# Inner layer norm of a four-layer graph network: statistics from ScalarE's running sums instead of VectorE's bn_stats, and T^T from VectorE's transposes

## The chip, the cores and the metric

The kernel runs on one core of a Trainium2 chip, as one launch. The metric is the device time of the launch in microseconds. An engine name stands for one of the core's five: TensorE (PE in the profile; its weight loads are PEld), VectorE (DVE), ScalarE (ACT), GpSimd (POOL) and SyncE (SP), which issues the DMA transfers.

## The reference

The input is x, 128 graphs of 64 nodes with 512 features, and adj, one 64 x 64 matrix for each graph, partly zero. All values are fp32. Four layers follow each other, each of the form x = x + L(relu(layernorm(x)), adj):

```python
# layer 0: two hypergraph convolutions with an inner layer norm
h = jax.nn.relu(hypergraph_conv(x, adj, W1, b1))      # 512 -> 1024
h = layer_norm(h, gamma, beta)                        # over the 1024: the "inner" one
y = hypergraph_conv(h, adj, W2, b2)                   # 1024 -> 512
return y + x
# layer 1: attention weights from s = (h @ w) @ a, out = A @ h @ w
# layer 2: softmax-like weights adj * exp(q k^T), times values
# layer 3: K = 3 hops
alpha_matrix = A * jnp.exp(e)
transition = alpha_matrix / (jnp.sum(alpha_matrix, axis=-1, keepdims=True) + 1e-12)
for k in range(Wk.shape[0]):
    H = H + Xk @ Wk[k] + bk[k]
    Xk = jnp.einsum('bij,bjd->bid', transition, Xk)
return jax.nn.relu(H)
```

The layer norms are (x - mean) / sqrt(variance + 1e-5), over the last axis.

## The kernel before

**Tiles and groups.** Two graphs make a tile of 128 rows; T = 4 tiles make a group, and there are 16 groups. Layers 0 and 1 run over all groups; their result goes to DRAM (xm), the weights of layers 2 and 3 replace the first ones in SBUF, and layers 2 and 3 run over all groups. A 64 x 64 matrix of two graphs stands in a 128 x 128 tile ("bd") as two blocks on the diagonal with zeros beside them.

**Products.** Large products go through `strassen` (L577), a form with seven products for eight over a pair of tiles, which emits four result quarters in the order (0,0), (1,1), (1,0), (0,1). Its matmuls stand on L595, those of the similar scheme of layer 2 on L818. A matmul of fp32 shows as two records in the profile.

**The inner layer norm (layer0, L661).** For a pair of tiles, `strassen` with W1 gives z, 128 x 1024 for each tile, in halves of 512. `emit_z` writes a half with VectorE (L615) and applies Relu in place on ScalarE (L707). When both halves of a tile are there, `norm_stats` (L504) runs bn_stats on each (L508) and bn_aggr (L509) on VectorE, and variance + eps and its power of -0.5 on GpSimd (L510, L511). ScalarE scales each half by that (L718; the mean is not subtracted, it is folded into W2). Each half is then transposed: ScalarE splits the words into 16-bit planes (L543), a DMA transposes them (L544) back onto z, ScalarE joins them in rT (L545). `strassen` with W2 (part "q") reads rT. The slots of z are two, so a pair's z must be read before the next pair's is written. The outer layer norms use the same `norm_stats`, through `pre_stats` (L514).

**T and T^T (layer3, L889).** VectorE makes T, the transition matrices of the four tiles, as the diagonal blocks of tr (L908). TensorE transposes each of the four 128 x 128 tiles (L915) into PSUM, ScalarE copies that to tt[:, :, 0, :] (L917). Then TensorE multiplies T by that (L921) and ScalarE copies the result to tt[:, :, 1, :] (L923), the transpose of T squared. The left multiplication `lm` (L936) multiplies h of one graph by its 64 columns of both planes at once, and ScalarE copies that into a3 (L940), the input of the product with the three hops' weights W3.

**What sets the order.** The program isn't written in the order of its text. Every operation is recorded in a `Graph` (L40) with an engine and an assumed cost. `run` (L82) then plays the five engines against each other: of the operations that can start first on an engine, the one with the lowest priority number goes. A priority is the group's time (`PERIOD1` or `PERIOD2` for each group), plus the work passed so far (`step`, times `STRETCH` of the layer), plus a constant of the part (`AT`; `part` sets it). Buffers of a tag (`SLOTS`, `TWO`) are handed out as this play finds them free. The resulting order is fixed in the program, and each engine keeps to it on the chip.

**Lines the prediction uses.** L469: setup products of Wq and Wk from tmp tiles. L534: left multiplication of a tile by a diagonal-block matrix. L679: the matrix M of layer 0. L731: y of layer 0. L844: scores of layer 2. L879, L882: its values and the reciprocal of the row sums. L525: the outer norm's ACTIVATE. L372: a dot product along a row, with VectorE's accumulator. L668: the 0/1 matrix of adj. L387 and the lines before it: sums of weights for `strassen`.

Of the kernel before, what the change touches and what calls it, by code (L numbers as in the profile page):

```python
# [18 lines left out]
T = 4  # L19
# [142 lines left out]
def tile_adj_preln_d4(  # L162
# [25 lines left out]
        ([("tmp", [P, D], 4), ("mB", [P, T, C + 1], 1)], [("s3", [P, 3, 6, P], 1)]),  # L188
        ([("z", [P, DH], 2)], [("hT", [P, KD, T * P], 1)]),
        ([("rT", [P, KH, P], 3)], [("a3", [P, 3 * KD, P], 2)]),  # L190
        ([("s2", [P, 3, 4, P], 1), ("s1", [P, 3, 2, P], 2)], [("vu", [P, 2, D + 1], 2), ("tt", [P, T, 2, P], 1)]),
        ([("y", [P, D], 2)], [("qT", [P, 2, 2 * P], 2)]),
        ([("mT", [P, KD, P], 3)], [("a3", [P, 3 * KD, P], 1)]),
        ([("row", [P, D], 5)], [("sh", [P, 4, 2, 2 * P], 1), ("q", [P, D], 1)]),
# [72 lines left out]
    def quad(b):  # L267
# [1 line left out]

    STRETCH, PERIOD1, PERIOD2 = (2.01, 1.52, 3.8, 3.15), 99.32, 100.99
    AT = {
        "x0": -1000.31, "apart": -0.04, "w1": -1140.59, "b1": -730.1, "w2": -692.69, "w": 166.49, "c1": -856.63,
        "l0": -580.98, "c2": -741.75, "l1": 111.32, "c": 219.34, "g0": -1134.91, "g1": -1116.26, "g2": -755.63,
        "g3": -850.44, "g": -1126.24, "l3": 28.03, "wg": 119.55, "w3": 191.39, "last": -98.19, "load1": -120.84,
        "load2": -92.69, "m": -52.0, "h0": -37.33, "p0": -2.35, "z0": -2.26, "q0": 25.57, "y0": -29.58, "h1": -39.25,
        "p1": -17.85, "z1": 10.94, "q1": 12.3, "y1": 27.38, "s": -11.54, "t0": 62.66, "e0": -103.04, "t1": 54.99,
        "e1": -32.68, "hT": -26.23, "sh": 50.82, "lq": 16.73, "pt": 40.17, "v": -3.1, "pv": -184.92, "s3": 16.54,
        "tt": 62.29, "a0": 61.26, "b0": -39.87, "a1": 81.07, "b1_": 65.71,  # L280
    }

    def part(name):
# [377 lines left out]
    def layer0(g):  # L661
# [28 lines left out]
        for t0 in (0, 2):  # L690
            mh, zs, ys, rTs, k = [], [], [], [], t0 // 2
            part(f"h{k}")
            for t in (t0, t0 + 1):
                xx = xt[g, t]
                h = pre_ln(g, t)
                pool(1.43, lambda xx=xx, h=h: nc.gpsimd.tensor_add(xx.t, xx.t, h.t), [h, xx], [xx])
                pool(1.39, lambda xx=xx: nc.gpsimd.tensor_add(xx.t, xx.t, b2_b.t), [xx, b2_b], [xx])
                mh.append(left_mul_T(h, lambda t=t: M.t[:, t, :], Mr, "mT"))
                zs.append(Buf("z"))
                ys.append(Buf("y"))  # L700
                rTs.append(Buf("rT"))
                step(0.9)

            def emit_z(i, j, p, u, v, t0=t0, zs=zs):
                z, cols, t = zs[i], slice(j * D, (j + 1) * D), t0 + i
                scaled(lambda: z.t[:, cols], (z, j), lambda: rd.t[:, t:t + 1], [rd], lambda: b1_b[j].t, [b1_b[j]], p, u, v, D)
                act(0.63, lambda: nc.scalar.activation(z.t[:, cols], z.t[:, cols], AF.Relu), [(z, j)], [(z, j)])  # L707

            part(f"p{k}")
            strassen(lambda i, j, mh=mh: mh[i].t[:, 2 * j:2 * j + 2, :], {(i, j): [mh[i]] for i in range(2) for j in range(2)},  # L710
                     W1, 2, D, "s1", emit_z)
            part(f"z{k}")
            for i in range(2):
                z, rT = zs[i], rTs[i]
                rs = norm_stats(lambda k, z=z: z.t[:, k * D:(k + 1) * D], 2, [(z, 0), (z, 1)])[1]
                for j in range(2):
                    half = lambda z=z, j=j: z.t[:, j * D:(j + 1) * D]
                    act(0.7, lambda half=half, rs=rs: nc.scalar.activation(half(), half(), AF.Copy, scale=rs.t), [(z, j), rs], [(z, j)])  # L718
                    transposed(half, [(z, j)], Buf("tmp"), half, [(z, j)], lambda rT=rT, j=j: rT.t[:, j * KD:(j + 1) * KD, :], [(rT, j)])
                    step(0.1)  # L720

            def emit_y(i, j, p, u, v, ys=ys):
                biased(ys[i], j, p, u, v, lambda: bw2_b.t, bw2_b)

            part(f"q{k}")
            strassen(lambda i, j, rTs=rTs: rTs[i].t[:, j * KD:(j + 1) * KD, :], {(i, j): [(rTs[i], j)] for i in range(2) for j in range(2)},
                     W2, 4, D // 2, "s2", emit_y)
            part(f"y{k}")
            for i in range(2):
                xx, y, pf, t = xt[g, t0 + i], ys[i], Buf("ps"), t0 + i  # L730
                pe(c_mm(512, 1), lambda y=y, pf=pf, t=t: nc.tensor.matmul(pf.t, M.t[:, t, :], y.t, start=True, stop=True), [(y, 0), (y, 1), *Mr], [pf])  # L731
                dve(0.75, lambda pf=pf, xx=xx, t=t: nc.vector.scalar_tensor_tensor(
                    xx.t, pf.t, rd.t[:, t:t + 1], xx.t, op0=ALU.mult, op1=ALU.add), [pf, rd, xx], [xx])
                step(0.9)
# [154 lines left out]
    def layer3(g):  # L889
# [16 lines left out]
        dve(0.18, lambda: nc.vector.reciprocal(rn.t, dn.t), [dn], [rn])  # L906
        for s in HALVES:
            dve(0.42, lambda s=s: nc.vector.tensor_mul(tr.t[s, :, s], z.t[s], rn.t[s, :, None].to_broadcast([C, T, C])), [z, rn], [(tr, s.start)])  # L908
        trk, pt, p2 = [(tr, 0), (tr, C)], Buf("ps"), Buf("ps")

        part("tt")

        def mt():
            for t in range(T):
                nc.tensor.transpose(quad(pt)[:, t, :], tr.t[:, t, :], ident)  # L915
        pe(KD * TR, mt, trk, [pt])
        act(0.59, lambda: nc.scalar.copy(tt.t[:, :, 0, :], quad(pt)), [pt], [(tt, 0)])  # L917

        def m2():
            for t in range(T):  # L920
                nc.tensor.matmul(quad(p2)[:, t, :], tr.t[:, t, :], tt.t[:, t, 0, :], start=True, stop=True)  # L921
        pe(c_mm(128, T), m2, [*trk, (tt, 0)], [p2])
        act(0.59, lambda: nc.scalar.copy(tt.t[:, :, 1, :], quad(p2)), [p2], [(tt, 1)])  # L923
        step(2.0)
        for t0 in (0, 2):
            part("a0" if t0 == 0 else "a1")
            for t in (t0, t0 + 1):
                h, b, back = pre_ln(g, t, stats[t]), a3[t], Buf("q")
                transposed(lambda h=h: h.t, [h], Buf("o"), lambda back=back: back.t, [back], lambda b=b: b.t[:, :KD, :], [(b, 0)])

                pq = [Buf("ps"), Buf("ps")]

                def lm(h=h, pq=pq, t=t):
                    for c in range(KD):
                        for i, half in enumerate(HALVES):
                            nc.tensor.matmul(quad(pq[i])[:, c, :], h.t[half, c * P:(c + 1) * P], tt.t[half, t, :, half],  # L936
                                             start=True, stop=True)
                pe(c_mm(128, KD) + 0.2, lm, [h, (tt, 0), (tt, 1)], pq)
                for i, half in enumerate(HALVES):
                    act(0.59, lambda pq=pq, b=b, i=i, half=half: nc.scalar.copy(  # L940
                        b.t[:, KD:, half].rearrange("p (j c) k -> p c j k", j=2),
                        pq[i].t.rearrange("p (c j k) -> p c j k", c=KD, j=2)), [pq[i]], [(b, 1 + i)])
                step(1.0)
# [131 lines left out]
```

## Time and profile before

| | |
|---|---|
| time, median of 3 runs (lowest, highest) | 2401.43 us (2398.42, 2402.01) |
| span of the profiled run | 2395.1 us |
| granted TensorE clock in it | 0.998 |
| bn_stats of z: busy, number | 86.2 us, 128 |
| bn_stats of x: busy, number | 174.1 us, 256 |
| TensorE's transposes of T: number, median | 64, 273 ns |
| ScalarE's copies of T^T: number, mean | 16, 585 ns |

The page gives busy time, share of the span and number of instructions of each engine; below that the span in 40 slices, a digit being the busy share in tenths. The durations of matmuls overlap, since they are pipelined and their ends are modelled: how long a matmul holds TensorE is read from the starts of neighbours. A group of instructions is one line, engine and operation with its tiles; after the bar stand its busy time, the mean of one, and the engine's idle time before it with what ended most of that. In a list of waits, the numbers are the total in us, how often, and the longest.

### The profile page before, as it was taken

To read this page: it belongs to the slowest core of one execution; us is meant where nothing else is said; L and a number is where in the kernel's file an instruction comes from. 1 tells how busy PE (TensorE), PEld (TensorE's weight loads), DVE (VectorE), ACT (ScalarE), POOL (GpSimd) and SP (SyncE) were. 2 spreads that over 40 slices of the span, in tenths; PEclk is the share of its full clock that TensorE was granted. 3 is DMA by queue.
4 is the path that set the end of the run, shared out by engine and by line. 5 is a ranking of instruction groups with operands and counts; after the bars stand their busy time and mean duration, and the time that the engine had idled before them with its cause. 6 is when DMAs were issued, how large, how long until landed. Compare 5 with 4: busy or idle time off the path is not lost.

```text
span 2395.1 us, 33543 instructions
## 1 busy us (share of the span) xinstructions
PE 2356.3 (98%) x11930; PEld 1855.0 (77%) x11930; DVE 1721.2 (72%) x3676; ACT 1263.5 (53%) x1754; POOL 938.2 (39%) x1450
## 2 busy tenths in 40 slices
PE   7999999999999999999999999999999999999999
PEld 3576677776777776777778888888888888888887
DVE  7887878787878787877878556666666666666664
ACT  2666565566565566565745445544445444454431
POOL 5234455434455434455344333333333333333321
PEclk9999999999999999999999999999999999999999
DMA  7232222232223222222532232222322222222211
GB/s 242 54 80 47 65 68 71 68 78 51 65 66 73 67 80 52 61 67 77 146 89 62 66 74 55 69 56 58 78 64 60 66 50 71 73 56 64 52 42 36
DMA packets 335928, 168.78 MB, mean 70 GB/s; under 512 B 284688, under 2 KB 290832, under 8 KB 335760
## 3 DMA queue, kind: packets, MB, share of 16 engines
q1 hardware_dynamic: 335760, 166.63, 28.0%
q8 instruction: 94, 1.54, 0.3%
q14 instruction: 74, 0.61, 0.1%
HBM read 64.76 MB, written 34.70 MB: 42 GB/s over the span
## 4 chain that ended last, share of the span: by engine, by line
PE 84%; DVE 6%; DMA 4%; ACT 2%; POOL 2%; issue 2%; SPq 0%; DVEq 0%; POOLq 0%; ACTq 0%
PE ps L595 60%; PE ps L818 11%; PE ps L534 4%; PE ps L936 2%; PE ps L731 2%; PE ps L879 2%; DVE s_s_vu_tt L869 1%; DMA x<-xm 1%; PE ps L844 1%; ACT o L543 1%; DVE bd L854 1%; ACT h L525 1%; POOL u L867 1%; POOL rs L511 1%; DVE st L508 1%
## 5 line engine op out<-in xcount | busy, mean ns | idle before, releaser
L525 ACT ACTIVATE h<-x,nm,rs 128x512 f32<-128x512 f32 x384 | 307.1, 813 | 456.5 <-POOL nm L518 455.3
L595 PE MATMUL ps<-wb_mem,rT_a 128*128 128x256 f32 x2056 | 476.8, 380 | 1.7 <-DVE z_hT L615 0.9
L595 PEld LDWEIGHTS ps<-wb_mem,rT_a 128*128 128x128 f32 x2056 | 386.5, 190 | 74.8 <-issue 20.3
L510 POOL TENSOR_SCALAR rs<-mv 128x1 f32<-128x1 f32 x320 | 101.5, 317 | 534.2 <-DVE mv L509 452.9
L595 PE MATMUL ps<-wb_mem,s_s_vu_tt 128*128 128x256 f32 x1152 | 275.0, 379 | 0.2 <-DVE s_s_vu_tt L587 0.2
L595 PE MATMUL ps<-wb_mem,tmp_mB_s 128*128 128x256 f32 x1152 | 261.3, 379 | 0.2 <-DVE tmp_mB_s L587 0.2
L595 PEld LDWEIGHTS ps<-wb_mem,s_s_vu_tt 128*128 128x128 f32 x1152 | 218.5, 190 | 43.1 <-issue 10.5
L595 PE MATMUL ps<-wb_mem,mT_a 128*128 128x256 f32 x1016 | 240.7, 380 | 1.8 <-ACT u L563 1.3
L595 PEld LDWEIGHTS ps<-wb_mem,tmp_mB_s 128*128 128x128 f32 x1152 | 217.6, 190 | 29.6 <-DVE tmp_mB_s L587 0.6
L595 PE MATMUL ps<-wa_mem,mT_a 128*128 128x512 f32 x512 | 238.0, 593 | 2.1 <-DVE u L567 2.1
L949 POOL TENSOR_TENSOR u<-u,bk_b 128x256 f32<-128x256 f32 x96 | 76.2, 799 | 352.3 <-DVE u L567 292.6
L511 POOL TENSOR_TENSOR rs<-rs,mhalf 128x1 f32<-128x1 f32 x320 | 202.9, 634 | 26.6
L595 PEld LDWEIGHTS ps<-wb_mem,mT_a 128*128 128x128 f32 x1016 | 190.6, 190 | 28.6 <-ACT u L563 1.5
L508 DVE BATCH_NORM_STATS2 st<-x 128x6 f32<-128x512 f32 x256 | 174.1, 680 | 32.4 <-DMA x<-xm 30.8
L595 PE MATMUL ps<-wa_mem,s_s_vu_tt 128*128 128x512 f32 x384 | 182.9, 599 | 1.0 <-ACT c_b L453 0.6
L595 PEld LDWEIGHTS ps<-wa_mem,mT_a 128*128 128x128 f32 x512 | 96.0, 190 | 105.4 <-issue 92.5
L565 DVE TENSOR_TENSOR u<-ps,u 128x256 f32<-128x256 f32 (+1 forms) x160 | 84.4, 527 | 112.1 <-PE ps L595 84.6
L623 POOL TENSOR_TENSOR u<-u,row_sh_q 128x256 f32<-128x256 f32 x96 | 70.9, 746 | 235.0 <-DVE u L565 205.9
L545 ACT COPY rT_a<-z_hT 128x1024 uint16<-128x1024 uint16 x128 | 144.3, 1161 | 4.4 <-DMA z_hT<-tmp_mB_s 4.2
L534 PEld LDWEIGHTS ps<-bd,h 128*128 128x128 f32 x1024 | 129.0, 192 | 16.1 <-issue 8.6
L707 ACT ACTIVATE z_hT<-z_hT 128x512 f32<-128x512 f32 x128 | 79.8, 625 | 116.7 <-DVE z_hT L615 116.6
L563 ACT COPY u<-ps 128x256 f32<-128x256 f32 (+1 forms) x160 | 72.5, 453 | 129.7 <-PE ps L818 71.5
(172 smaller groups left out, 4317.1 us busy)
## 6 DMA issues: line engine op xcount, KB each, us to landing
x<-in_x_dram SPq DMA_DIRECT2D x64, 256.0 KB, 2.8
xm<-x SPq DMA_DIRECT2D x64, 256.0 KB, 2.0
x<-xm SPq DMA_DIRECT2D x64, 256.0 KB, 2.7
out_dram<-x SPq DMA_DIRECT2D x64, 256.0 KB, 2.2
adj<-in_adj_dram SPq DMA_DIRECT2D x32, 256.0 KB, 4.1
rw<-row SPq DMA_DIRECT2D x96, 64.0 KB, 2.8
wb_mem<-in_Wk_dram SPq DMA_DIRECT2D x6, 512.0 KB, 4.4
wa_mem<-in_W1T_dram SPq DMA_DIRECT2D x2, 1024.0 KB, 5.9
```

What stands on the lines that cost most here:

```text
L508: dve(0.69, lambda i=i: nc.vector.bn_stats(st.t[:, i, :], src(i)), [r[i]], [(st, i)])
L510: pool(0.3, lambda: nc.gpsimd.tensor_scalar_add(rs.t, mv.t[:, 1:2], EPS), [mv], [rs])
L511: pool(0.65, lambda: nc.gpsimd.tensor_tensor(rs.t, rs.t, mhalf, ALU.pow), [rs], [rs])
L525: act(0.82, lambda: nc.scalar.activation(h.t, xx.t, AF.Relu, bias=nm.t, scale=rs.t), [xx, nm, rs], [h])
L534: nc.tensor.matmul(quad(p)[:, c, :], h.t[:, c * P:(c + 1) * P], rhs(), start=True, stop=True)
L545: act(1.16, lambda: nc.scalar.copy(u16(dst()).rearrange("p c (k q) -> p c k q", q=2), u16(back()).rearrange("p (q c r) -> p c r q", q=2, c ...
L563: act(n / 1200 + 0.17, lambda: nc.scalar.copy(at(0)(), p1.t[:, :n]), [p1], [(U, 0)])
L565: dve(c_v(n), lambda: nc.vector.tensor_add(at(1)(), p2.t[:, :n], at(0)()), [p2, (U, 0)], [(U, 1)])
L595: nc.tensor.matmul(p.t[:, :n], lhs()[:, c, :], rhs(c), start=first and c == 0, stop=c == kc - 1, skip_group_check=True)
L707: act(0.63, lambda: nc.scalar.activation(z.t[:, cols], z.t[:, cols], AF.Relu), [(z, j)], [(z, j)])
L818: nc.tensor.matmul(pair(p.t)[:, o, :], a, b, start=first and o == 0 and c == 0, stop=c == 1, skip_group_check=True)
L949: pool(0.88, lambda: nc.gpsimd.tensor_add(U.t[:, iv], U.t[:, u[1]], add()), [u, ka], [v])
```

## The change

The statistics of the inner norm move from VectorE to ScalarE and GpSimd. The Relu of each half of z now also gives the half's sum (`accum_out`). GpSimd adds the two sums and divides by -1024, which is minus the mean. Two Squares on ScalarE, with that as the bias, write their result to a scrap tile and give the sums of squared distances; GpSimd adds these, divides, adds eps and takes the power -0.5. VectorE's bn_stats and bn_aggr on z are gone; those of the outer norms stay.

T^T is made by VectorE: a 64 x 64 block is transposed as four blocks of 32 x 32, the two off the diagonal changing places, for four tiles in one instruction. It goes from SBUF to SBUF, without TensorE, PSUM and ScalarE. tt now holds 64 columns for a tile, both graphs below each other, instead of 128, and has two slots instead of one in the same room. The product that gives the transpose of T squared has 64 columns instead of 128.

The planner's constants (STRETCH, PERIOD1, PERIOD2 and all of AT) are other numbers, so the order of the whole program differs.

```diff
-        ([("s2", [P, 3, 4, P], 1), ("s1", [P, 3, 2, P], 2)], [("vu", [P, 2, D + 1], 2), ("tt", [P, T, 2, P], 1)]),
+        ([("s2", [P, 3, 4, P], 1), ("s1", [P, 3, 2, P], 2)], [("vu", [P, 2, D + 1], 2), ("tt", [P, T, 2, C], 2)]),
...
-    STRETCH, PERIOD1, PERIOD2 = (2.01, 1.52, 3.8, 3.15), 99.32, 100.99
+    STRETCH, PERIOD1, PERIOD2 = (2.04, 0.7, 3.87, 2.94), 97.36, 106.92
...
+            zsum = [Buf("col"), Buf("col")]
...
-                act(0.63, lambda: nc.scalar.activation(z.t[:, cols], z.t[:, cols], AF.Relu), [(z, j)], [(z, j)])
+                act(0.65, lambda: nc.scalar.activation(z.t[:, cols], z.t[:, cols], AF.Relu, accum_out=zsum[i].t[:, j:j + 1]), [(z, j)], [(z, j), (zsum[i], j)])
...
-                rs = norm_stats(lambda k, z=z: z.t[:, k * D:(k + 1) * D], 2, [(z, 0), (z, 1)])[1]
+                sm, nm, rs = zsum[i], Buf("nm"), Buf("rs")
+                pool(0.3, lambda sm=sm, nm=nm: nc.gpsimd.tensor_add(nm.t, sm.t[:, 0:1], sm.t[:, 1:2]), [(sm, 0), (sm, 1)], [nm])
+                pool(0.3, lambda nm=nm: nc.gpsimd.tensor_scalar(nm.t, nm.t, -1.0 / DH, None, op0=ALU.mult), [nm], [nm])
+                for j in range(2):
+                    junk = Buf("o")
+                    act(0.65, lambda z=z, j=j, sm=sm, nm=nm, junk=junk: nc.scalar.activation(
+                        junk.t, z.t[:, j * D:(j + 1) * D], AF.Square, bias=nm.t, accum_out=sm.t[:, 2 + j:3 + j]), [(z, j), nm], [junk, (sm, 2 + j)])
+                pool(0.3, lambda sm=sm, rs=rs: nc.gpsimd.tensor_add(rs.t, sm.t[:, 2:3], sm.t[:, 3:4]), [(sm, 2), (sm, 3)], [rs])
+                pool(0.3, lambda rs=rs: nc.gpsimd.tensor_scalar(rs.t, rs.t, 1.0 / DH, EPS, op0=ALU.mult, op1=ALU.add), [rs], [rs])
+                pool(0.65, lambda rs=rs: nc.gpsimd.tensor_tensor(rs.t, rs.t, mhalf, ALU.pow), [rs], [rs])
...
-        trk, pt, p2 = [(tr, 0), (tr, C)], Buf("ps"), Buf("ps")
+        trk, p2 = [(tr, 0), (tr, C)], Buf("ps")
+        B = C // 2
+        def blocks(s):
+            for i in range(2):
+                for j in range(2):
+                    nc.vector.transpose(tt.t[s.start + j * B:s.start + (j + 1) * B, :, 0, i * B:(i + 1) * B],
+                                        tr.t[s.start + i * B:s.start + (i + 1) * B, :, s.start + j * B:s.start + (j + 1) * B])
+        for i, s in enumerate(HALVES):
+            dve(1.2, lambda s=s: blocks(s), [(tr, s.start)], [(tt, 2 + i)])
...
-        def mt():
-            for t in range(T):
-                nc.tensor.transpose(quad(pt)[:, t, :], tr.t[:, t, :], ident)
-        pe(KD * TR, mt, trk, [pt])
-        act(0.59, lambda: nc.scalar.copy(tt.t[:, :, 0, :], quad(pt)), [pt], [(tt, 0)])
...
-                nc.tensor.matmul(quad(p2)[:, t, :], tr.t[:, t, :], tt.t[:, t, 0, :], start=True, stop=True)
-        pe(c_mm(128, T), m2, [*trk, (tt, 0)], [p2])
-        act(0.59, lambda: nc.scalar.copy(tt.t[:, :, 1, :], quad(p2)), [p2], [(tt, 1)])
+                nc.tensor.matmul(p2.t[:, t * C:(t + 1) * C], tr.t[:, t, :], tt.t[:, t, 0, :], start=True, stop=True)
+        pe(c_mm(64, T), m2, [*trk, (tt, 2), (tt, 3)], [p2])
+        act(0.38, lambda: nc.scalar.copy(tt.t[:, :, 1, :], p2.t[:, :T * C].rearrange("p (t c) -> p t c", t=T)), [p2], [(tt, 1)])
...
-                            nc.tensor.matmul(quad(pq[i])[:, c, :], h.t[half, c * P:(c + 1) * P], tt.t[half, t, :, half],
+                            nc.tensor.matmul(quad(pq[i])[:, c, :], h.t[half, c * P:(c + 1) * P], tt.t[half, t, :, :],
```

In the changed kernel the product with T stands on L937 and the new transposes on L928.

## The prediction

> **What bounds the kernel now.** I first read the page's head: busy shares and the 40 slices.
>
> ```profile
> span 2395.1 us, 33543 instructions
> PE 2356.3 (98%) x11930; PEld 1855.0 (77%) x11930; DVE 1721.2 (72%) x3676; ACT 1263.5 (53%) x1754; POOL 938.2 (39%) x1450
> ...
> PE   7999999999999999999999999999999999999999
> ```
>
> TensorE works nearly without a break; VectorE, which the change relieves most, is at 72%. So a saving on VectorE counts only where VectorE makes TensorE wait. To see where that happens I asked for busy time by stretch: start-up, layers 0 and 1, their hand-over to layers 2 and 3, these, and the end.
>
> ```profile
> 0.00:100.00 100.00, 83.41 (x280) 43.94 (x281) 78.49 (x152) 35.81 (x53) 45.62 (x64) 0.98 0.54 166
> 100.00:1150.00 1050.00, 1049.73 (x4415) 759.50 (x4414) 836.42 (x1855) 648.41 (x915) 482.57 (x750) 1.00 0.27 66
> 1150.00:1300.00 150.00, 140.15 (x806) 118.49 (x804) 118.55 (x250) 78.35 (x106) 64.47 (x102) 0.99 0.39 104
> 1300.00:2290.00 990.00, 985.51 (x5894) 850.22 (x5892) 632.07 (x1310) 475.47 (x645) 324.78 (x506) 1.00 0.28 64
> 2290.00:2396.00 106.00, 97.54 (x543) 82.86 (x541) 55.66 (x113) 25.48 (x36) 20.75 (x30) 0.99 0.13 34
> ```
>
> After the stretch's length the columns are PE, PEld, DVE, ACT and POOL busy time. TensorE's idle time is 16.6, 0.3, 9.9, 4.5 and 8.5 us. In layers 0 and 1 it is 0.3 us of 1050: there the new statistics can win nothing, only lose. What a change can win lies in TensorE's own instructions, at the start, at the hand-over and at the end. The list of TensorE's waits agrees: for VectorE's T (L908) it waited once, 1.9 us, and longest for a first load.
>
> ```profile
> PE ps L469 <- DMA tmp_mB_s<-in_Wk_dram: 10.4, 2, 9.5
> PE ps L879 <- DVE ve L882: 4.6, 15, 0.3
> ...
> PE ps L915 <- DVE bd L908: 1.9, 1, 1.9
> ```
>
> The rows that the change touches, from the groups (busy us, mean ns of one, then idle time before):
>
> ```profile
> L508 DVE BATCH_NORM_STATS2 st<-z_hT 128x6 f32<-128x512 f32 x128 | 86.2, 675 | 22.4 <-ACT z_hT L707 22.4
> L707 ACT ACTIVATE z_hT<-z_hT 128x512 f32<-128x512 f32 x128 | 79.8, 625 | 116.7 <-DVE z_hT L615 116.6
> L718 ACT ACTIVATE z_hT<-z_hT,rs 128x512 f32<-128x512 f32 x128 | 91.7, 718 | 50.8 <-POOL rs L511 48.8
> ```
>
> And the timeline of TensorE in one group of layer 3 (start, duration), transposes first:
>
> ```profile
> 1687.38 0.60 PE L915 MATMUL ps<-ident,bd 128*128 128x128 f32 x4
> 1687.81 2.75 PE L595 MATMUL ps<-wb_mem,rT_a 128*128 128x256 f32 x12
> 1690.40 1.05 PE L921 MATMUL ps<-s_s_vu_tt,bd 128*128 128x128 f32 x8
> ```
>
> Durations of matmuls overlap, starts do not: the four transposes hold TensorE from 1687.38 to 1687.81, 0.43 us.
>
> **What the Trainium skill says.** "TensorE: Matmul & The Clock Gate", Part 1: warm matmuls start N / 2.4 GHz + 2.5 ns apart, and an idle array begins at half clock. An fp32 product here is two records, and for N = 256 they start 216 ns apart, twice the stated 109; so fp32 pays two passes per record. The first 12 records, 8.2 us from 9.52 to 17.70, show the cold clock. "ScalarE: Activation LUTs", What ACT_TABLE_LOAD costs: 186 ns + 0.833 N with immediates, 93 ns more for each pointer operand. For N = 512 that is 612, 705, 798; the trace has 625 (L707), 718 (L718), 813 (L525). It agrees. "VectorE: DVE Perf Modes", Two Vector instructions with no wait between them: an instruction whose input or output starts in another group of 32 partitions is held until the earlier ones are done. The new transposes change groups from one to the next, so I let them run end to start; no row of before shows one.
>
> **Part by part: the statistics.** Out go 128 bn_stats x 0.68 us = 86 us and 64 bn_aggr x 0.18 = 12 us of VectorE. In come 128 Squares on ScalarE, one pointer operand like L718, 0.72 each = 92 us, and for 256 sums an unknown price: VectorE's read of an accumulator took 0.08 (L372); I take 0.1 and keep 0 and 0.2. ScalarE gains 92 + 26 = 118 us over some 1180 us (L707's rows run to the hand-over), from about 62% to 72% busy. GpSimd gets three more one-column operations per z tile, 64 x 3 x 0.3 = 58 us, from 46% to 51%. No engine becomes fuller than TensorE.
>
> The wait it adds: ScalarE's Square waits for GpSimd's mean, which waits for ScalarE's last Relu; behind it in ScalarE's queue stand the copies of mT and of the next z. For W2's first product the path from the last W1 product gets longer by two GpSimd operations (0.65 with gaps), up to four Squares (2.9) and one more GpSimd operation (0.3), less bn_stats and bn_aggr (0.9): 3.0 us. How much room is there? In TensorE's order before, between the last W1 product of a pair of tiles and the first W2 product of that pair stand 12.9 us (625.77 to 638.68 in the group I followed) and 13.1 us for the other pair, and TensorE waited for neither. In the changed order I count, with a W1 or W2 product at 1.72, a y product at 0.86, a W product at 0.86 and a left multiplication at 0.89: five W2, two y, three W1 products and one left multiplication, 16.4 us, and for the other pair 30.3. So 3.0 longer stands against 3.5 more room, with the old slack on top: cost 0. The 98 us taken from VectorE lie beside TensorE's work as well: gain 0.
>
> **T^T.** TensorE loses 64 transposes at 0.109 (0.43 / 4): **7.0 us**, all on the path. The multiplication behind them now has N = 64 for 128. L679 with N = 65 held TensorE 0.83 us for eight records (629.21 to 630.04), L921 with N = 128 0.90 (1690.40 to 1691.30): 0.07 per group, 1 us in all, if anything; I take 0. ScalarE loses 16 copies x 0.59 and has shorter second ones, hidden.
>
> VectorE gets 128 transposes of 32 x 128 elements, eight per group, all between T and the multiplication. From below: L668 (64x256, 0.31) less 128 elements at 0.96 GHz, 0.18. From above: a whole 64x256 operation, 0.42 (L908). L908 fits 256 / 0.96 GHz + 0.15; with 128 elements that is 0.29, which I take: 2.3 us per group. T was ready 18.5 us after the last attention product (L879) in most groups, but 20.05, 19.43, 19.78 and 19.02 in four. Two VectorE operations leave that stretch in the new order (0.25 net of ScalarE's Exp, which they covered), so the multiplication can start at that number + 2.05. TensorE's work ahead of it in the new order is two left multiplications of layer 3 (1.09 each), three layer-2 products (1.73), a score product (0.62) and five W3 products (2.6): 20.95 us. Four groups are late, by 1.15, 0.53, 0.88 and 0.12: **+2.7 us**. At 0.18 a transpose it is 0.4, at 0.42 it is 12.9.
>
> First group: 22.0 us of work against 22.6 + 2.05, a wait of 2.6 where there was one of 1.9: **+0.7**. Last group: the new order has 17.75 us ahead of the multiplication, the chain needed 20.9 + 2.05; 5.2 of waiting where about 1.9 was: **+3.3**.
>
> **The new order.** Planner constants move everything. At the start W1 (two transfers of 1 MB, landing at 5.6 and 8.2 us) stood ahead of the first Wq and Wk tiles, which landed at 8.8 and 9.4; now x, Wq, Wk come first. A first transfer needs 2.3 us and 0.63 per 256 KB (from these landings), so Wk is there at 5.0 and TensorE starts 4.4 us earlier. The waits of 1.1 and 0.8 us before the first W1 product look avoidable too, since Wq and Wk of the last tiles no longer queue behind W2. W1 then lands near 14, and its sums are needed near 35. I take **-6**, with 0 and -8 as ends. Hand-over and the rest: same kinds of work in similar order, 0, with 5 us either way.
>
> Sum: -7.0 - 6 + 2.7 + 0.7 + 3.3 = -6.3; 2401.4 - 6.3 = **2395.0**.
>
> **Rivals.** A, the T^T wait eats it: transposes at 0.42, +10 on the sum, 2405; or the start gives its 6 us back, 2401. For it: T was late by more than its usual 18.5 in four groups. Against: the wait must arise in most groups. 0.27, mostly no change. B, the ScalarE chain surfaces in layers 0 and 1: 0.5 us in each of 32 pairs is +16, **2411**, slower. For it: ScalarE is in order and idle time before L718 was already ended by GpSimd (48.8 us). Against: the counted room. 0.10. C, VectorE's relief shortens start and hand-over too, where it was 78% and 79% busy: a third of the 26 us idle there, -9, 2386. 0.10. The forecast has 0.53; about a fifth of it lies within 0.2% (above 2396.6).
>
> Range: 2385 (C) to 2406 (A), leaving out B and some of the rest. Faster 0.42 + 0.10 + 0.03 of A = 0.55; same 0.11 + 0.20 = 0.31; slower B and what is left of A, 0.14.
>
> **What would show it.** TensorE 64 records fewer, 11866, still idle under 2 us from 100 to 1150 us; first matmul near 5 us; ScalarE up by about 110 us, VectorE down by 98 - 37 = 61; L937 waiting for the transposes in a few groups and in the last. Waits of W2's first products for rT, ended by ScalarE's copies, would prove me wrong (B), as would L937 waiting a microsecond in every group (A).

## The result, and the profile after

The changed kernel takes 2420.59 us (median of 4 runs, 2416.65 to 2422.07) against 2400.38 for the kernel before beside it. The ratio is 1.0082, with a 95% interval of 1.0065 to 1.0099. The forecast was 2395.0, range 2385 to 2406, so the change went the other way: 20 us slower, where 6 us were to be won.

The head of the page of the changed kernel:

```profile
span 2420.3 us, 33900 instructions
PE 2363.5 (98%) x11866; PEld 1850.6 (76%) x11866; DVE 1714.8 (71%) x3612; ACT 1350.6 (56%) x2122; POOL 988.7 (41%) x1642
```

TensorE has its 64 records fewer. ScalarE gained 87 us (about 110 expected) and GpSimd 51 (58 expected). VectorE does not fit: it lost 98 us of statistics and got 39 us of transposes, and yet its busy time fell by only 6. Something else on VectorE became longer. The same stretches as before (length, then PE, PEld, DVE, ACT and POOL busy time):

```profile
0.00:100.00 100.00, 86.03 (x294) 47.33 (x295) 78.46 (x153) 43.63 (x79) 46.10 (x73) 0.97 0.52 166
100.00:1150.00 1050.00, 1036.52 (x4347) 745.79 (x4346) 782.40 (x1642) 730.65 (x1251) 537.28 (x921) 1.00 0.27 66
1150.00:1300.00 150.00, 136.82 (x748) 112.26 (x747) 112.96 (x233) 81.76 (x120) 56.84 (x95) 0.99 0.40 101
1300.00:2290.00 990.00, 983.56 (x5806) 841.92 (x5806) 670.78 (x1436) 461.26 (x626) 322.14 (x517) 1.00 0.27 63
2290.00:2421.00 131.00, 120.57 (x677) 103.34 (x676) 70.15 (x151) 33.31 (x49) 26.36 (x36) 0.97 0.16 40
```

In layers 0 and 1, 100 to 1150 us, TensorE was idle for 0.3 us and now for 13.5. That is the largest item. Its waits in the changed kernel (in all, times, longest):

```profile
PE ps L595 <- DVE s_s_vu_tt L587: 12.2, 14, 2.3
PE ps L937 <- DVE s_s_vu_tt L928: 6.7, 6, 4.0
PE ps L595 <- ACT u L563: 6.6, 3, 5.3
PE ps L469 <- DMA tmp_mB_s<-in_Wk_dram: 6.1, 1, 6.1
...
PE ps L595 <- DVE u L567: 3.8, 1, 3.8
PE ps L595 <- ACT rT_a L545: 2.8, 1, 2.8
```

The first line is new: in 14 groups a product of `strassen` waits for VectorE's sums (L587). Nearly everything of layers 0 and 1 that went wrong is in it. The wait for rT behind ScalarE's copies (L545), which rival B feared, came once.

For a full account I took TensorE's idle time as the gap between the starts of two neighbouring matmuls less the pitch that a matmul of that width shows where nothing waits (0.216 us for 256 columns, 0.429 for 512). Before, it is 59.6 us, after, 95.2. Of the 35.6 more, about 16 fall between 100 and 1100 us, 7 between 1100 and 1300, 8 between 1300 and 2300, and 5 in the end. Against that stand 7.0 us of transposes gone and a first matmul at 6.08 for 9.52 us: 35.6 - 7.0 - 3.4 = 25.2, the difference of the two profiled spans (2420.3 and 2395.1).

Not all of that is waiting. For about 22 us of the changed kernel, against 7 before, the trace shows the granted clock at one half, and the matmuls of 256 and 512 columns in these stretches come 6.3 us later than their pitch, against 1.8. So some 4.5 of the 35.6 us are a slower clock.

**Why the sums are late.** The groups of VectorE's 128 x 512 sums of rT, first of the kernel before:

```profile
L587 DVE TENSOR_TENSOR s_s_vu_tt<-s_s_vu_tt,rT_a 128x512 f32<-128x512 f32 x32 | 22.4, 699 | 1.2 <-ACT rT_a L545 0.2
L587 DVE TENSOR_TENSOR rT_a<-rT_a 128x512 f32<-128x512 f32 x32 | 21.9, 685 | 0.0
```

and of the changed kernel:

```profile
L587 DVE TENSOR_TENSOR s_s_vu_tt<-s_s_vu_tt,rT_a 128x512 f32<-128x512 f32 x32 | 33.8, 1056 | 0.7
L587 DVE TENSOR_TENSOR rT_a<-rT_a 128x512 f32<-128x512 f32 x32 | 33.7, 1052 | 0.0
```

The same instructions take half as long again in the mean. In the kernel before, none of the 128 sums of rT overlaps one of GpSimd's adds of h and b2 to x (L696, L697). In the changed one, 35 do by more than 0.1 us: the 11 that started ahead of the add took 0.66 us, the 24 that came second 1.64 to 1.77. The timeline of one group shows what lies beside them (start, duration):

```profile
680.20 0.66 DVE L587 TENSOR_TENSOR s_s_vu_tt<-rT_a 128x512 f32<-128x512 f32 x1
680.40 1.59 POOL L696 TENSOR_TENSOR x<-x,h 128x512 f32<-128x512 f32 x1 [0.93 <-ACT h L525]
680.89 1.64 DVE L587 TENSOR_TENSOR s_s_vu_tt<-s_s_vu_tt,rT_a 128x512 f32<-128x512 f32 x1
...
682.07 1.60 POOL L697 TENSOR_TENSOR x<-x,row_sh_q 128x512 f32<-128x512 f32 x1
...
682.46 1.76 DVE L587 TENSOR_TENSOR rT_a<-rT_a 128x512 f32<-128x512 f32 x1
...
684.14 0.68 DVE L587 TENSOR_TENSOR s_s_vu_tt<-rT_a,s_s_vu_tt 128x512 f32<-128x512 f32 x1
684.74 0.41 DVE L587 TENSOR_TENSOR s_s_vu_tt<-mT_a 128x256 f32<-128x256 f32 x1
685.19 0.42 DVE L587 TENSOR_TENSOR s_s_vu_tt<-s_s_vu_tt,mT_a 128x256 f32<-128x256 f32 x1
...
685.66 0.70 PE L595 MATMUL ps<-wa_mem,s_s_vu_tt 128*128 128x512 f32 x1 [0.69 <-DVE s_s_vu_tt L587]
```

Two sums take 1.64 and 1.76 us where they took 0.68, just those that start while an add (L696, L697) is at work. Behind the four sums of rT stand, in VectorE's order, the two sums of mT that W1's second product reads; that product waits. The collision ran both ways: GpSimd's adds, which each start while a sum is at work, took 1.59 and 1.60 us here, 1.27 undisturbed. The Trainium skill states this ("SBUF — State Buffer", Who interferes with whom): a VectorE instruction with two SBUF inputs contends with a GpSimd instruction that reads SBUF, not with one that only writes it, and the one that comes second is blocked until the first is done. The trace agrees: the second sum starts at 680.89 and ends at 682.53, which is the end of L696 (681.99) plus 0.54, most of a free sum's length.

The kernel before shows the other half of it. There 56 of VectorE's bn_stats, which read one tile, overlap one of these adds by more than 0.1 us, and they take 0.67 us at the median, against 0.68 for the others. One of them:

```profile
620.13 1.27 POOL L697 TENSOR_TENSOR x<-x,row_sh_q 128x512 f32<-128x512 f32 x1
...
620.23 0.69 DVE L508 BATCH_NORM_STATS2 st<-z_hT 128x6 f32<-128x512 f32 x1 [0.77 <-ACT z_hT L707]
```

So most of what stood beside the adds on VectorE was harmless before, and the new order puts sums of two tiles there.

### The profile page after: what moved, and what is told of

It reads as the page before. It is cut to its first block, busy times and chain, and to the rows that moved or that the text cites. A ratio compares the mean times of both kernels' runs of the same rounds, so it can differ in the third digit from the quotient of the medians.

```text
span 2420.3 us, 33900 instructions
## 1 busy us (share of the span) xinstructions
PE 2363.5 (98%) x11866; PEld 1850.6 (76%) x11866; DVE 1714.8 (71%) x3612; ACT 1350.6 (56%) x2122; POOL 988.7 (41%) x1642
## 4 chain that ended last, share of the span: by engine, by line
PE 80%; DVE 9%; DMA 5%; POOL 3%; ACT 2%; issue 2%; SPq 0%; DVEq 0%; POOLq 0%; ACTq 0%
PE ps L595 53%; PE ps L830 14%; PE ps L534 4%; PE ps L891 2%; DVE s_s_vu_tt L587 2%; PE ps L743 2%; PE ps L952 2%; PE ps L856 1%; DMA rw<-row 1%; POOL rs L511 1%; DVE rT_a L587 1%; DMA x<-xm 1%; DVE st L508 1%; POOL nm L518 1%; DMA out_dram<-x 1%
## 5 line engine op out<-in xcount | busy, mean ns | idle before, releaser
L595 PE MATMUL ps<-wb_mem,rT_a 128*128 128x256 f32 x2080 | 484.6, 381 | 4.0 <-ACT rT_a L545 2.8
L595 PEld LDWEIGHTS ps<-wb_mem,rT_a 128*128 128x128 f32 x2080 | 393.7, 191 | 74.3 <-issue 15.0
L595 PE MATMUL ps<-wb_mem,s_s_vu_tt 128*128 128x256 f32 x1152 | 280.2, 380 | 1.2 <-DVE s_s_vu_tt L587 0.5
L510 POOL TENSOR_SCALAR rs<-mv 128x1 f32<-128x1 f32 x256 | 83.7, 327 | 453.6 <-DVE mv L509 429.3
L595 PE MATMUL ps<-wa_mem,s_s_vu_tt 128*128 128x512 f32 x384 | 184.8, 605 | 12.2 <-DVE s_s_vu_tt L587 11.7
L511 POOL TENSOR_TENSOR rs<-rs,mhalf 128x1 f32<-128x1 f32 x256 | 166.2, 649 | 21.2
L545 ACT COPY rT_a<-z_hT 128x1024 uint16<-128x1024 uint16 x128 | 147.6, 1159 | 28.5 <-DMA z_hT<-tmp_mB_s 28.3
L623 POOL TENSOR_TENSOR u<-u,row_sh_q 128x256 f32<-128x256 f32 x96 | 79.5, 842 | 205.5 <-DVE u L565 180.5
L543 ACT COPY o<-h 128x1024 uint16<-128x1024 uint16 x128 | 133.7, 1045 | 4.7 <-DMA row_sh_q<-o 2.2
```

The costliest lines, as they stand in the source:

```text
L510: pool(0.3, lambda: nc.gpsimd.tensor_scalar_add(rs.t, mv.t[:, 1:2], EPS), [mv], [rs])
L511: pool(0.65, lambda: nc.gpsimd.tensor_tensor(rs.t, rs.t, mhalf, ALU.pow), [rs], [rs])
L543: act(1.05, lambda: nc.scalar.copy(u16(planes.t).rearrange("p (q c) -> p q c", q=2), u16(src()).rearrange("p (c q) -> p q c", q=2)), ksrc, ...
L545: act(1.16, lambda: nc.scalar.copy(u16(dst()).rearrange("p c (k q) -> p c k q", q=2), u16(back()).rearrange("p (q c r) -> p c r q", q=2, c ...
L595: nc.tensor.matmul(p.t[:, :n], lhs()[:, c, :], rhs(c), start=first and c == 0, stop=c == kc - 1, skip_group_check=True)
L623: pool(0.75, lambda: nc.gpsimd.tensor_add(U.t[:, iv], U.t[:, iu], row()[:, cols]), [u, krow], [v])
```

## The experiments

Each ran beside the kernel before, whose medians were 2397.44 to 2400.8 us. A ratio is to the kernel before, with its 95% interval.

**1 to 4: parts of the change.** First only the lines of the statistics:

```diff
-                rs = norm_stats(lambda k, z=z: z.t[:, k * D:(k + 1) * D], 2, [(z, 0), (z, 1)])[1]
+                sm, nm, rs = zsum[i], Buf("nm"), Buf("rs")
...
+                        junk.t, z.t[:, j * D:(j + 1) * D], AF.Square, bias=nm.t, accum_out=sm.t[:, 2 + j:3 + j]), [(z, j), nm], [junk, (sm, 2 + j)])
```

> The kernel before with the new statistics alone (planner constants and T^T as before). Theory O (the new constants, so the new order, cost the time): 2396 to 2404 us, no repeated wait of TensorE in layers 0 and 1. Theory S (the statistics' longer path and ScalarE's load cost it): 2415 or more, TensorE idle 15 us or more between 100 and 1150 us, with waits ended by ScalarE's copies. Theory C (VectorE and GpSimd slow each other, and statistics on GpSimd add to it): 2405 to 2412, VectorE's sums L587 longer than before.

Measured 2505.4 us, ratio 1.0441 [1.0424, 1.0459]. Its waits:

```profile
PE ps L595 <- ACT rT_a L545: 51.8, 14, 4.7
```

With the old constants the longer path to rT does surface, by 3.7 us in 14 groups: rival B, in another order than the one it was feared for.

Second, only T^T by VectorE, with the old constants:

```diff
-        pe(KD * TR, mt, trk, [pt])
+            dve(1.2, lambda s=s: blocks(s), [(tr, s.start)], [(tt, 2 + i)])
```

> The kernel before with T^T by VectorE alone (constants and statistics as before). Theory O: the 7.0 us of TensorE's transposes are saved and some waits of the product with T come in, 2393 to 2400 us. Theory T (the wait for T^T costs more than the transposes): 2402 or more, TensorE waiting for the transposes over half a microsecond in most groups.

Measured 2417.36 us, ratio 1.0078 [1.0063, 1.0094]. Layers 0 and 1 are as before (0.4 us idle from 100 to 1150); the loss lies in the waits of layers 2 and 3:

```profile
PE ps L925 <- DVE s_s_vu_tt L916: 5.9, 3, 4.4
PE ps L595 <- DVE u L567: 5.4, 1, 5.4
PE ps L595 <- ACT mT_a L944: 5.2, 1, 5.2
```

Third, only the constants (these and all of AT); fourth, statistics and constants:

```diff
-    STRETCH, PERIOD1, PERIOD2 = (2.01, 1.52, 3.8, 3.15), 99.32, 100.99
+    STRETCH, PERIOD1, PERIOD2 = (2.04, 0.7, 3.87, 2.94), 97.36, 106.92
```

> The kernel before with the new planner constants alone, its operations untouched. Theory O: 2412 us or more, with a wait of some 0.85 us per group in layers 0 and 1 for VectorE's sums of mT (L587), as in the changed kernel. Theories S and T: 2390 to 2400 us.

> New statistics and new constants, T^T by TensorE as before. Theory O: within 4 us of the run with the constants alone plus what the statistics alone cost; the changed kernel's loss in layers 0 and 1 (16 us of TensorE idle) is all here. Theory T: 2400 us or less, since the T^T wait is gone.

Measured 2507.93 us (1.0445 [1.0429, 1.0461]) and 2448.15 us (1.0202 [1.0188, 1.0217]). The parts don't add up: 105, 17 and 108 us alone, 20 together. A set of constants fits the operations that it was made for, and a part with the wrong set seems to tell mostly of the misfit. What can be used is the waits of the fourth, whose layers 0 and 1 are those of the changed kernel without anything of T^T:

```profile
PE ps L927 <- DVE bd L920: 12.3, 1, 12.3
PE ps L595 <- DVE s_s_vu_tt L587: 12.1, 14, 2.3
```

The 12 us behind L587 come with the statistics and the order together, not with T^T. The lengths of the sums of rT say the same: 0.69 and 0.68 us in the mean with the statistics alone (run 1), 0.70 and 0.72 with the constants alone (run 3), 1.06 and 1.05 with both (run 4). The wait for L587 alone would mislead: run 3 has 19.8 us of it in 19, with sums of nearly the old length, so the sums of mT are late there for another reason, which I did not follow. From here on, but for runs 9 and 11 to 13, I left the order alone and altered only how long a suspect takes.

**5 and 6: GpSimd's adds cut, in the changed kernel and in the one before.** Both leave out x + h + b2 on all but 8 of 512 columns.

```diff
-                pool(1.43, lambda xx=xx, h=h: nc.gpsimd.tensor_add(xx.t, xx.t, h.t), [h, xx], [xx])
-                pool(1.39, lambda xx=xx: nc.gpsimd.tensor_add(xx.t, xx.t, b2_b.t), [xx, b2_b], [xx])
+                pool(1.43, lambda xx=xx, h=h: nc.gpsimd.tensor_add(xx.t[:, :8], xx.t[:, :8], h.t[:, :8]), [h, xx], [xx])
+                pool(1.39, lambda xx=xx: nc.gpsimd.tensor_add(xx.t[:, :8], xx.t[:, :8], b2_b.t[:, :8]), [xx, b2_b], [xx])
```

> The changed kernel with its order untouched, but GpSimd's two adds of layer 0 (x+h, L696, and +b2, L697) work on 8 of 512 columns: it leaves out the rest of x+h+b2. Theory 'contention' (VectorE's sums of rT take 1.0 to 1.8 us instead of 0.69 while GpSimd adds, and W1's second product waits behind them): the 128x512 sums of rT come back to about 0.69 us, the wait of L595 for VectorE's L587 (12 us in 14) goes, TensorE's idle time in layers 0 and 1 goes from 15 us to 2 to 5 us, and the time falls by 10 to 15 us to 2405 to 2411. Theory 'order' (mT's sum merely stands late in VectorE's order, whatever GpSimd does): the waits stay and the time is 2418 to 2422. Theory 'ScalarE is too full': the same as 'order', with the waits for rT (L545) and u (L563).

> The kernel before with the same cut (L696 and L697 of layer 0 on 8 of 512 columns; it leaves out the rest of x+h+b2), as the control of the run above. Theory 'contention': in the old order the adds seldom meet the sums of rT (33 of 128, 3 us in all), and TensorE idles 1 us in layers 0 and 1 together, so the cut brings 0 to 2 us: 2398 to 2400. If the cut brings 8 us or more here too, its gain in the changed kernel says nothing on the change.

Measured 2396.41 us (0.9983 [0.9975, 0.9991]) and 2394.82 us (0.9980 [0.9972, 0.9989]). The changed kernel gains 24 us, more than the 10 to 15 expected; the control gains 4.7, also more than expected, because the adds cost both kernels time in the start-up that I hadn't counted (idle time in the first 100 us falls from 14.1 to 8.7 and from 14.5 to 9.1). The control's expectation also speaks of 33 sums of rT that meet the adds in the old order. In the trace none does: the long sums there (`s_s_vu_tt<-rT_a,s_s_vu_tt`, 765 ns in the mean) stand beside another reading instruction of GpSimd, L772, and stay as long with the cut (764). Net of the control, 19 of the 20 us of the loss go with the adds. Layers 0 and 1 of the changed kernel with the cut:

```profile
100.00:1150.00 1050.00, 1048.50 (x4413) 757.68 (x4412) 763.00 (x1666) 740.43 (x1273) 407.02 (x931) 1.00 0.27 67
```

TensorE's 13.5 us of idle time are down to 1.5. VectorE's busy time in the whole run fell from 1714.8 to 1672.3: these 42 us, which went with the adds, are most of the 55 that VectorE's relief fell short of. But the cut takes 2.1 us of work per tile off GpSimd too (two adds of 1.37, now 0.31). Was it the reads, or the work?

**7: ScalarE's Squares cut** to 8 columns. It leaves out most of the squared distances.

```diff
-                        junk.t, z.t[:, j * D:(j + 1) * D], AF.Square, ...
+                        junk.t[:, :8], z.t[:, j * D:j * D + 8], AF.Square, ...
```

> The changed kernel with its order untouched, but ScalarE's Squares on 8 of 512 columns: it leaves out most of the squared distances, so rs is another number. It takes 64 x about 0.5 us x 2 = 55 to 65 us of work off ScalarE. Theory 'ScalarE is too full or its chain to rs is too long': the waits in layers 0 and 1 go, 2405 to 2412. Theory 'contention': rs comes 1 us earlier in a chain that has some microseconds to spare, and the waits behind the sums of rT stay: 2415 to 2421.

Measured 2418.9 us, 1.0083 [1.0064, 1.0101]. The wait for L587 stays:

```profile
PE ps L595 <- DVE s_s_vu_tt L587: 11.2, 14, 1.8
```

ScalarE's load, the forecast's main worry for the statistics, is not the cause.

**10: GpSimd as long at work, without reading.**

```diff
-                pool(1.39, lambda xx=xx: nc.gpsimd.tensor_add(xx.t, xx.t, b2_b.t), [xx, b2_b], [xx])
+                pool(1.39, lambda xx=xx: [nc.gpsimd.tensor_add(xx.t[:, :8], xx.t[:, :8], b2_b.t[:, :8]), *(nc.gpsimd.memset(xx.t[:, 8:], v) for v in (0.5, 1.0))], [xx, b2_b], [xx])
```

(and so for L696; x + h + b2 is left out but for 8 columns, with a constant in place of the rest)

> The changed kernel with its order untouched; GpSimd's two adds of layer 0 (L696, L697) work on 8 of 512 columns and are each followed by two memsets of the other 504 columns of x, so that GpSimd is as long at work (estimate: 0.36 + 2 x 0.52 and 0.20 + 2 x 0.52 us, from the 8-column adds of the run with the adds cut and the setup's memsets, against 1.27 of an undisturbed add) but hardly reads SBUF meanwhile. It leaves out x+h+b2 but for 8 columns, and puts a constant in their place. Theory 'VectorE's sums and GpSimd's reads of SBUF get in each other's way': the sums of rT stay at about 0.69 us and the time is that of the run with the adds cut, 2394 to 2400. Theory 'GpSimd is too long at work and what follows it is late': as the changed kernel, 2416 to 2422, with short sums of rT. If memsets slow the sums as adds do: as the changed kernel, with long sums.

Measured 2396.3 us, 0.9984 [0.9977, 0.9992]: the time of run 5. GpSimd's groups and VectorE's:

```profile
L697 POOL MEMSET x<- 128x504 f32 x128 | 66.2, 517 | 3.7
L697 POOL TENSOR_TENSOR x<-x,row_sh_q 128x8 f32<-128x8 f32 x64 | 15.8, 246 | 8.9 <-DMA row_sh_q<-in_b_dram 8.9
```

```profile
L587 DVE TENSOR_TENSOR s_s_vu_tt<-s_s_vu_tt,rT_a 128x512 f32<-128x512 f32 x32 | 22.4, 700 | 0.7
L587 DVE TENSOR_TENSOR rT_a<-rT_a 128x512 f32<-128x512 f32 x32 | 21.9, 684 | 0.0
```

With two memsets and a short add, 0.246 + 2 x 0.517 = 1.28 us (1.41 for L696), GpSimd works as long as with an undisturbed add, and the sums are back at 0.69: 38 of them overlap a memset and take 0.69 us at the median. So it is GpSimd's reading, as the skill has it, and not GpSimd's time. That VectorE's instruction must have two SBUF inputs is the page's statement; no run varied it, and the bn_stats above agree with it.

**8: the transposes of T cut** to one tile of four. It leaves out three quarters of T^T.

```diff
-                    nc.vector.transpose(tt.t[s.start + j * B:s.start + (j + 1) * B, :, 0, i * B:(i + 1) * B],
+                    nc.vector.transpose(tt.t[s.start + j * B:s.start + (j + 1) * B, 0:1, 0, i * B:(i + 1) * B],
```

> The changed kernel with its order untouched, but each of the eight 32-row transposes of T does one of its four tiles: it leaves out three quarters of T^T. T^T is then there some 1.2 to 1.8 us sooner in each group. Theory 'T^T waits cost what the trace shows' (L937 waits for L928 6.7 to 7.9 us in all, 4.1 of it in the first group): the waits go but for 1 to 3 us in the first group, and 3 to 6 us of time come back: 2414 to 2418. Theory 'they are made up for elsewhere' (what TensorE waits here it would wait further on): below 2 us, 2418 to 2421.

Measured 2413.15 us, 1.0052 [1.0039, 1.0066]: 7.4 us less than the changed kernel. The waits for the transposes:

```profile
PE ps L937 <- DVE s_s_vu_tt L928: 2.2, 3, 1.8
```

They were 6.7 in 6. So 4.5 us of waits went, and the other 3 us are not accounted for: the runs of each kernel spread over 5 to 7 us, and most of the idle time that went lies at the hand-over (1100 to 1300 us). By the time VectorE's T^T, in front of the product that needs it, costs what the TensorE transposes cost; by the waits at least two thirds of it.

**9: one of the two adds moved.** b2 is added later in GpSimd's order, all other orders kept:

```diff
-                pool(1.39, lambda xx=xx: nc.gpsimd.tensor_add(xx.t, xx.t, b2_b.t), [xx, b2_b], [xx])
+                pool(1.39, lambda: None, [xx, b2_b], [xx])
...
+                if (i, j) == (0, 0):
+                    o, xs = G.ops[-1], [xt[g, t0], xt[g, t0 + 1]]
+                    def late(fn=o.fn, xs=xs):
+                        fn()
+                        for xx in xs:
+                            nc.gpsimd.tensor_add(xx.t, xx.t, b2_b.t)
+                    o.fn = late
```

> The changed kernel with every engine's order kept but for one thing: GpSimd's adds of b2 (half of its long adds in layer 0) are put later in its own order, behind the first output block of W2's products of the same pair (L625), away from VectorE's sums of rT; nothing is left out. Theory 'contention': the sums of rT that met the second add come back to 0.69 us, about half of the 25 us of excess goes, and with it half or more of the 0.9 to 1.9 us that TensorE waits in each group of layers 0 and 1: 2408 to 2414. If the length of the sums is not what TensorE waits for: 2418 to 2422.

Measured 2439.21 us, 1.0172 [1.0152, 1.0193]: 19 us slower than the changed kernel, a miss. The sums that met L697 are free again (rT_a<-rT_a 0.68 us, from 1.05), those that meet L696 are not (1.03 us), and the wait for L587 is down from 12.2 us to 1.9. Other waits took its place:

```profile
PE ps L595 <- ACT u L563: 16.9, 16, 5.3
PE ps L595 <- ACT mT_a L536: 6.8, 13, 1.3
```

and ScalarE's groups show whose they are:

```profile
L730 ACT ACTIVATE z_hT<-z_hT,rs 128x512 f32<-128x512 f32 x128 | 91.8, 720 | 46.9 <-POOL rs L727 46.9
L723 ACT ACTIVATE o<-z_hT,nm 128x512 f32<-128x512 f32 x128 | 90.9, 712 | 40.3 <-POOL nm L720 40.2
```

In the changed kernel these idle times were 11.7 and 6.4 us. The two late adds now stand ahead of GpSimd's one-column operations for the mean and rs; ScalarE waits for those, and TensorE for ScalarE's copies (L563, L536), which stand behind them in ScalarE's order. This is the price of the new statistics that the forecast looked for: GpSimd is now in the path, and a long add can't be put just anywhere.

**11 to 13: a planner that knows of the collision.** A VectorE sum of `strassen` that starts beside a long GpSimd add is planned longer, the changed operations have costs from the trace (those of Relu and Square, 0.82 and 0.90 us, too long: with their accumulator reads they start 0.63 and 0.71 us apart), and the constants are searched anew for each of three sets of operations: those before, those after, and T^T alone.

```diff
+            if o.eng == "POOL" and o.cost >= 0.7:
+                self.pl = (t, t + o.cost)
+            if o.two:
+                a_, b_ = getattr(self, "pl", (0, 0)); ov = max(0, min(b_ - t, o.cost / 0.42)) if a_ <= t else 0
+                o.cost = o.cost + 0.58 * ov
```

> The operations of the kernel before, nothing left out; the planner lengthens a VectorE sum of strassen by the time that it would stand beside a long GpSimd add, and STRETCH, PERIOD and AT are searched anew for that. It is the control for the two runs beside it. TensorE idles 60 us in the kernel before, 15 of them at the start and some 16 at the hand-over, and without the long adds it was 5 us faster. If a planner that knows of the collision is worth something by itself: 2385 to 2396. If the kernel before had no collisions to lose, a new order brings nothing or costs what the planner doesn't see: 2397 to 2415.

> All operations of the changed kernel, nothing left out; the same planner, which also takes the measured durations of Relu and Square with their accumulator reads (0.82 and 0.90 us) and of the transposes (1.26 for four), and constants searched anew. If the loss lay in the order alone (collision of the sums of rT with GpSimd's adds), and the change itself brings its 7 us of TensorE work: it is below the changed kernel by 20 us or more and 4 to 8 us below the control beside it. If the change leaves ScalarE and GpSimd so full that any order of it waits: 5 us or more above the control, whatever the order. The wait for VectorE's L587 in front of W1's second product should be below 4 us in either case.

> The T^T half of the change alone (the statistics stay bn_stats on VectorE), nothing left out; the same planner, constants searched anew. It saves the same 7 us of TensorE work without more work for ScalarE and GpSimd in layers 0 and 1. If T^T by VectorE is the half that is worth having: 3 to 8 us below the control beside it. If VectorE's 2.5 us per group in front of the product with T eat the 7 us in any order: within 2 us of the control or above.

Measured 2406.86 (1.0032 [1.0020, 1.0044]), 2409.68 (1.0045 [1.0032, 1.0058]) and 2412.97 us (1.0056 [1.0043, 1.0068]). None beats the kernel before. The changed operations gain 11 us by the new order: TensorE's idle time from 100 to 1150 us is 5.0 us for 13.5. The control lost 6, so the planner still misses other things, and the comparison is with it: the changed kernel is 2.8 us above (the intervals overlap), T^T alone 6 us. The 7 us of TensorE's transposes are not to be seen in either. Waits of the replanned changed kernel:

```profile
PE ps L600 <- ACT u L568: 8.0, 3, 5.3
PE ps L942 <- DVE s_s_vu_tt L933: 4.8, 5, 2.5
...
PE ps L600 <- DVE s_s_vu_tt L592: 2.5, 4, 1.3
```

(lines are 5 higher here). The wait for the sums is small, as expected, though one of the four sums still meets an add in 13 of 32 cases:

```profile
L592 DVE TENSOR_TENSOR rT_a<-rT_a 128x512 f32<-128x512 f32 x32 | 35.9, 1121 | 0.0
```

So a long sum costs TensorE little where no product waits behind it. The waits for T^T are little less than they were, and the one of 5.3 us in the last group is as it was.

## Why the prediction was wrong, step by step

**The step that failed** is the pricing of the statistics: "3.0 longer stands against 3.5 more room, with the old slack on top: cost 0", together with "Hand-over and the rest: same kinds of work in similar order, 0". The first looked for the cost on the path to rT only, and there the counted room did hold (2.8 us, once). The cost came by another road: the new order puts GpSimd's adds of x beside VectorE's sums of rT, and the sums of mT behind these. It measured about 16 us in layers 0 and 1, of which runs 5 and 10 take 14 away. I had priced VectorE by counting its instructions at the durations of the kernel before, without asking which GpSimd instruction would run beside each. The profile of before showed those adds, at 1.29 us, and even some sums lengthened by another reading instruction of GpSimd (L772; mean 765 ns for 685), and the skill's page names the pairs that collide. That the order would put them side by side could not be read from that profile, only from the new order.

**Point by point.** TensorE's 64 transposes: 7.0 us, right, and given back. ScalarE's additions: the record of a Square lasts 0.71 us, against 0.72. An accumulator read was priced at 0.1, and that was right: in the kernel before, the instruction behind a Relu, where it waits for nothing, starts 0.52 us after it (51 cases), with the read 0.63 us (37 cases). What was wrong is the sum of 0.82 for a Square with its read. Squares start 0.706 us apart, because ScalarE's records overlap by some 0.1 us where no read stands between them (L718 and L730 last 0.72 and start the next instruction after 0.62), so the length of a record is too high a price. ScalarE's rise is 87 us for 110. VectorE was to fall by 61 us and fell by 6, as told. Rival B, by its sign the right side, had the wrong cause: not ScalarE's chain (run 7). It was true only with the old constants (run 1) and where GpSimd's order was touched (run 9).

A transpose: 0.303 us against 0.29, right. The rate in that estimate fits VectorE's own sums: 0.42 us for 256 columns, 0.68 for 512, 0.95 for 768, about 1.03 ns a column. The eight of a group start 0.31 to 0.32 us apart, so they do run end to start, as the forecast let them, 2.5 us in all.

```profile
L928 DVE STREAM_TRANSPOSE s_s_vu_tt<-bd 32x128 f32<-32x128 f32 x128 | 38.7, 303 | 2.0
```

The waits of the product with T: forecast were 2.7 us in four groups, 2.6 in the first and 5.2 in the last, 10.5 in all. By gaps they were 7.9, in other places: 4.1 in the first group, 3.4 in five others, 0.4 in the last. In the last group a product waits 5.3 us for ScalarE's copy L563 instead, which the order puts behind the outer norms' h. That wait costs more than its length:

```profile
2356.22 5.07 PE L595 MATMUL ps<-wb_mem,mT_a 128*128 128x256 f32 x12 [5.34 <-ACT u L563]
2361.12 2.75 PE L595 MATMUL ps<-wb_mem,tmp_mB_s 128*128 128x256 f32 x12
```

From 2353.9 to 2360.7 us the trace shows the clock at one half, and the first twelve records take 4.90 us from start to start where the next twelve take 2.59: 2.3 us more. The size of the waits for T^T was about right, and with the one in the last group they eat the 7 us: rival A's mechanism, though not its "microsecond in every group".

The start: -6 forecast, first matmul at 6.08 us for "near 5" and 0.4 us less idle time in the first 100 us, so -3.8. Its bound of -8 had assumed that the short waits there go; GpSimd's adds hold 5.4 us there in both kernels (runs 5 and 6).

The hand-over: 0 with 5 either way; it was 7 us more between 1100 and 1300 (15.6 and 22.7). Without the adds it is 18.7 before and 17.5 after. So the difference goes with them, 5 us of it in the changed kernel; that the kernel before has 3 us more without them is not explained.

Without the adds (runs 5 and 6) the two kernels differ by 1.6 us, and the account closes: by the gaps, -7.0 of transposes, -3.8 for the first matmul, +7.7 in layers 2 and 3, +4.9 at the end, and small items. So even without these adds the forecast's -6.3 would have been missed: layers 2 and 3 and the end cost 12.6 us where the T^T terms had 6.7, and the start gave 3.8 for 6.

**What stays open.** Why the wait of 5.3 us in the last group comes back in every order with the new T^T that was planned for it (after, run 12, run 13) wasn't tried. Whether an order exists in which the change wins its 7 us isn't known: the searches for runs 12 and 13 did not find one.

## What to carry to other kernels

An operation's price depends on what runs beside it: before calling VectorE's time free or fixed, list its instructions with two SBUF inputs and GpSimd's long reading ones, and check in the new order which of them meet and which product waits behind them. An instruction beside a long add may be harmless, as the bn_stats were, and what takes its place may not be. Constants of a scheduler belong to one set of operations; take a change apart by keeping its order and shortening one suspect, not by swapping halves under the wrong constants. And replace a suspect by something equally long that lacks the suspected property (memsets for adds): that tells the property from the time.

## What the runs showed of the hardware

A VectorE add of two 128 x 512 fp32 tiles in SBUF takes 0.68 us, and 1.64 to 1.77 where it starts beside a running GpSimd add of two such tiles. The GpSimd add takes 1.27 us, and 1.6 where it came second in the group shown. Beside GpSimd's memsets the VectorE add takes 0.69, and bn_stats, which reads one tile, keeps its 0.68 beside the adds.

Reading ScalarE's accumulator is a record of its own, 187 to 188 ns in the mean, which starts 0.1 us before its ACTIVATE is recorded as done. It delays the next instruction by about 0.1 us. A Relu with a copy behind it, first in the kernel before and then, with the read, in the changed one:

```profile
619.58 0.61 ACT L707 ACTIVATE z_hT<-z_hT 128x512 f32<-128x512 f32 x1
620.10 0.56 ACT L536 COPY mT_a<-ps 128x512 f32<-128x512 f32 x1
...
696.23 0.63 ACT L709 ACTIVATE z_hT<-z_hT 128x512 f32<-128x512 f32 x1 [1.30 <-DVE z_hT L615]
696.77 0.19 ACT L709 ACTIVATION_READ_ACCUMULATOR z_hT<-z_hT 128x1 f32 x1
696.86 0.57 ACT L536 COPY mT_a<-ps 128x512 f32<-128x512 f32 x1
```

Squares with a read behind each start 0.706 us apart, less than the two records together (0.90), and more than the 0.62 after which an ACTIVATE of that size without a read (L718, L730) starts the next instruction. Eight VectorE transposes of 32 rows by 128 fp32 columns, each with its input or its output in another group of rows than the one ahead, take 2.5 us.
